# A graph-attention step whose gathers are released from ten places of VectorE's program instead of six places of two engines

## The chip, the cores and the metric

One core of one Trainium2 chip runs the whole kernel. The metric is device time in microseconds, from launch to the last output row, and the time before is the median of three runs: 2590.57 us (2587.11 to 2598.71). The core has five engines with programs of their own: TensorE (matmuls; PE in the profile, PEld for its weight loads), VectorE (DVE), ScalarE (ACT), GpSimd (POOL) and SyncE (SP, which only issues DMAs here). Each works through its program in order; they meet at semaphores.

## The reference

There are 6250 nodes with 64 values each, and 206250 edges sorted by destination (`dst`), each with 64 attributes.

```python
Qh = (x @ Wq.T + bq).reshape(n, H, D)          # H = 4 heads of D = 16
Kh = (x @ Wk.T + bk).reshape(n, H, D)
Vh = (x @ Wv.T + bv).reshape(n, H, D)
Ee = (edge_attr @ We.T + be).reshape(-1, H, D)
score = (Kh[src] * Qh[dst] * (1.0 / np.sqrt(D)) * Ee).sum(-1)
score = jnp.exp(jnp.clip(score, -5.0, 5.0))
msg = Vh[src] * score[..., None]
wV = jax.ops.segment_sum(msg, dst, num_segments=n)
x = _layernorm(x + wV)
```

So for every edge a row of keys and values is picked by `src` (an irregular index), a row of queries by `dst` (a slowly growing one), and the messages are added up by `dst`.

## The kernel before

*Setup.* TensorE makes a table `kv_tab` in HBM with 128 floats (key and value) for each node, and a query table. The edges are cut into 1612 tiles of 128, the tiles into groups of 8 (`G`), the groups into 105 steps (`STEPS`): 97 steps of two groups, 16 tiles, and eight of one group at the end.

*Gathers.* For a tile of 128 edges `gather_kv` (L450) issues one indirect DMA from GpSimd (L452): it reads 128 indices, one in each partition, and brings 128 rows of `kv_tab` into the tile's column of one of five buffers `kvs` (`KVB`). Step s issues the gathers of step s + 4, whose buffer step s - 1 has just given up. Not all of a step's 16 tiles are gathered: the last two or three of the second group are "picked" (below), and in each sixth step one tile comes row by row through SyncE (`fetch_rows`, L617). That leaves 14, 13 or 12.

*Release.* The gathers' indices lie in `src_i` from the start. So that a gather is not issued at once, an engine copies the columns that are due from `src_i` to `due_i` (L593 on VectorE, L595 on ScalarE), and the gathers read `due_i`: the place of this copy in its engine's program decides when they may start. `PARTS` cuts a step's 16 tiles in six parts; parts 0 to 2 are copied by VectorE, parts 3 to 5 by ScalarE. GpSimd itself does nothing else in the loop.

*A step on the engines.* The order of each engine's program is written out by hand in the loop over s (L793 to L874); an engine does what concerns it in that order.

- VectorE: the two products of the scores (`products`, L680 and L681, in place over keys, queries and edge values), the sum over the picked rows (`picked`, L553; in each fifth step also L546), the sum over the heads and the clip (`scores`, L687 and L689), two additions into the destinations' ring (`add`, L730), the message (L697), then one-hot matrices: two `hot` (L525), the destinations' one-hot (L663), two more `hot` (another two in each fifth step); then now and then the closing of a block of output.
- ScalarE: the squares (L650) and the rest (L655) that make the queries' one-hot `to` out of `pb`, the exponential (L690), the bias of the edge values (L642), the split of the message in three bf16 parts (L700, then L710 twice, with a matmul L708 ahead of each), a copy of the turned picked rows (L563), the picked rows' keys and values (L580).
- TensorE: the previous step's sums over destinations (L716), small transposes (L515), the spread of the destinations over partitions (`spread`, L628, into `pb`), the picks (below), the edge values (`edges`, L441, 16 matmuls), L708, the picked rows through the weights (L573, L575), the queries (`queries`, L673, 16 matmuls).
- Picks: two tiles of a step (three in each fifth) are not gathered but made by TensorE: the `hot` matrices select rows of x in 2 x 25 matmuls for each tile (`picks`, L539), in 100 matmuls a step (150 in each fifth).

L680 of the next step needs L673's queries and L580's rows; L553 needs the last picks; L650 needs L628; L710 needs L708; the last `hot` of a step needs a buffer that 25 picks have read.

Of the kernel before, what the change touches and what calls it, by code (L numbers as in the profile page):

```python
# [21 lines left out]
G = 8  # L22
# [16 lines left out]
KVB = 5  # L39
# [14 lines left out]
def tiles_in(s):  # L54
    return sum(tiles_of(g) for g in groups_of(s))
# [8 lines left out]
LAST = NS - 8 - 1  # L64
PARTS = 0, 2, 4, 7, 9, 11, 16

# [48 lines left out]
def tile_gnn(ctx: ExitStack, tc: tile.TileContext, x, xT, wT, bias, beT, weT, eT, src, dst, dst_rows,  # L115
             src_rows, out):
    nc = tc.nc
# [345 lines left out]
    with tc.If(rv == 0) as branch:  # L463

        with tc.tile_pool(name="work", bufs=2) as work, \
# [115 lines left out]

            def gather(s, part):

                if s >= NS:
                    return
                t0, n = STEPS[s][0] * G, tiles_in(s)
                lo, hi = PARTS[part] * n // 16, PARTS[part + 1] * n // 16
                todo = [t for t in range(t0 + lo, t0 + hi) if not is_picked(t // G, t % G)
                        and not (is_rowed(s) and t - t0 == COLUMN)]
                if todo:  # L590
                    due = slice(todo[0], todo[-1] + 1)
                    if part < 3:
                        nc.vector.tensor_copy(due_i[:, due], src_i[:, due])  # L593
                    else:
                        nc.scalar.activation(due_i[:, due], src_i[:, due], AF.Copy)  # L595
                for t in todo:
                    gather_kv(t // G, t % G, due_i)
# [79 lines left out]
            def products(s):  # L677
                n = tiles_in(s)
                prod = work.tile([P, 2 * G, C], F32, name="prod", bufs=1)
                nc.vector.tensor_mul(prod[:, :n, :], kvs[s % KVB][:, :n, :C], PQ[s][:, :n, :])  # L680
                nc.vector.tensor_mul(prod[:, :n, :], prod[:, :n, :], PE[s][:, :n, :])  # L681
                return prod

            def scores(s, prod):
# [3 lines left out]
                                        axis=AX.X, op=OP.add)  # L688
                nc.vector.tensor_scalar(score, score, -5.0, 5.0, op0=OP.max, op1=OP.min)  # L689
                nc.scalar.activation(score, score, AF.Exp)  # L690
                return score
# [101 lines left out]
            for s in range(NS):  # L793
# [14 lines left out]
                prod = products(s)  # L808
                gather(s + KVB - 1, 0)
                picked(s - 1)  # L810
# [4 lines left out]
                score = scores(s, prod)  # L815
                gather(s + KVB - 1, 1)
                if more:
                    biases(s + 1)
                    onehot_rows_rest(nexts[0])
                if s:  # L820
                    add(s - 1)
                msg = message(s, score)
                gather(s + KVB - 1, 2)
                if nexts[1:]:
# [3 lines left out]
                minus(s, msg, 0)  # L828
                gather(s + KVB - 1, 3)
                if nexts[1:]:  # L830
                    onehot_rows_rest(nexts[1])
                hots(s, 1, 0)
                picks(s, 0, 1)
                picked_turned(s - 1)
                minus(s, msg, 1)
                gather(s + KVB - 1, 4)
                if not more:

                    close(B - 2)
                    spreads(B - 2)  # L840
                hots(s, 1, 1)
                picks(s, 1, 0)
                picked_kv(s - 1)
                gather(s + KVB - 1, 5)
                sources(s + 1, 1)
                sources(s + 2, 0)
                sources(s + 1, 2)
                if more:
                    rows_fetched(s + 1)
                    if nexts[0] * G % KEYS == 0:  # L850
                        keys(nexts[0] * G)
                    onehot_edges(s + 1)
                    queries(s + 1)
                picks(s, 1, 1)
                for h in range(2):
                    hots(s, 2, h)
                for h in range(2):
                    picks(s, 2, h)
                hots(s + 1, 0, 0)
                hots(s + 1, 0, 1)  # L860
                if more:

# [188 lines left out]
```

## Time and profile before

| | |
|---|---|
| median of 3 runs | 2590.57 us (2587.11 to 2598.71) |
| the profiled execution | 2600.91 us |
| its span, first to last instruction | 2598.9 us |
| mean granted TensorE clock | 0.877 |
| first start of L680 / last | 144.6 us / 2586.1 us |
| busy: TensorE, VectorE, GpSimd, ScalarE | 1975.9, 1633.1, 1308.6, 1037.3 us |

The profile shows one execution. A row such as `L452 POOL DMA_INDIRECT kv<-kv_tab,due_i x1325 | 1250.9, 944 | 1212.2 <-...` names line, engine, operation, what is written and read, how often; then busy time, mean ns of one, idle time of the engine just ahead of it, and what ended most of that. A row of the timeline has the start and the length in us, engine, line, operation, what it writes and reads, how many were merged, and in brackets the engine's idle time ahead of it with its releaser. "issue" is a wait that nothing in the profile explains; "remote" and "another core or an unknown queue" mean that a semaphore came, but not just after any instruction that sets it. GpSimd's row for a gather covers the making of its transfer, not the transfer.

### The profile page before, as it was taken

To read this page: it belongs to the slowest core of one execution; us is meant where nothing else is said; L and a number is where in the kernel's file an instruction comes from. 1 tells how busy PE (TensorE), PEld (TensorE's weight loads), DVE (VectorE), ACT (ScalarE), POOL (GpSimd) and SP (SyncE) were. 2 spreads that over 40 slices of the span, in tenths; PEclk is the share of its full clock that TensorE was granted. 3 is DMA by queue.
4 is the path that set the end of the run, shared out by engine and by line. 5 is a ranking of instruction groups with operands and counts; after the bars stand their busy time and mean duration, and the time that the engine had idled before them with its cause. 6 is when DMAs were issued, how large, how long until landed. Compare 5 with 4: busy or idle time off the path is not lost.

```text
span 2598.9 us, 48744 instructions
## 1 busy us (share of the span) xinstructions
PE 1975.9 (76%) x17255; PEld 1622.2 (62%) x17255; DVE 1633.1 (63%) x2106; ACT 1037.3 (40%) x1793; POOL 1308.6 (50%) x1396
## 2 busy tenths in 40 slices
PE   4587887777877877777777777877777877877884
PEld 4466666666766666666666666666666666656663
DVE  3366666566665766766656656566666665756774
ACT  1344333344343434433434334343444443433454
POOL 4335554545554545545554545555545554555442
PEclk9979888888988989888988888888988988889995
DMA  4312221212222222222222222222222222222221
GB/s 125 115 35 65 59 64 54 64 53 68 64 64 54 67 54 67 60 63 65 55 64 62 58 63 54 64 64 55 72 57 64 67 58 62 58 62 65 60 57 37
DMA packets 108379, 163.46 MB, mean 63 GB/s; under 512 B 68825, under 2 KB 71084, under 8 KB 108012
## 3 DMA queue, kind: packets, MB, share of 16 engines
q0 software_dynamic: 44288, 89.74, 13.1%
q1 hardware_dynamic: 63452, 69.51, 9.5%
q8 instruction: 137, 2.24, 0.4%
q10 hardware_dynamic: 384, 1.00, 0.2%
q14 instruction: 118, 0.97, 0.1%
HBM read 152.80 MB, written 7.33 MB: 62 GB/s over the span
## 4 chain that ended last, share of the span: by engine, by line
PE 50%; issue 15%; another core or an unknown queue 12%; ACT 10%; DVE 8%; POOL 5%; DMA 1%; DVEq 0%; SPq 0%; ACTq 0%; POOLq 0%
PE pick L539 22%; PE pe L441 7%; POOL kv L452 5%; PE pb L539 4%; PE pq L708 4%; PE small L716 3%; ACT msg L710 2%; PE pb L575 2%; DVE small L687 2%; ACT pe L642 2%; DVE prod L680 2%; PE pq L673 2%; PE pb L628 2%; DVE prod L681 2%
## 5 line engine op out<-in xcount | busy, mean ns | idle before, releaser
L452 POOL DMA_INDIRECT kv<-kv_tab,due_i x1325 | 1250.9, 944 | 1212.2 <-DVE due_i L593 427.2
L539 PEld LDWEIGHTS <-hot 128*128 128x128 bf16 x10650 | 980.9, 105 | 470.8 <-issue 404.3
L539 PE MATMUL pick<-parts,hot 128*128 128x192 bf16 x9700 | 1008.0, 261 | 240.9 <-issue 168.2
L525 DVE TENSOR_TENSOR hot<-small,block 128x3200 bf16<-128x3200 bf16 x426 | 755.9, 1814 | 40.4 <-PE pick L539 15.0
L650 ACT ACTIVATE to<-pb,minus_row 126x1024 bf16<-126x1024 f32 x202 | 224.3, 1111 | 912.4 <-PE pb L628 441.6
L680 DVE TENSOR_TENSOR prod<-kv,pq 128x1024 f32<-128x1024 f32 (+2 forms) x105 | 123.6, 1177 | 419.4 <-ACT kv L580 94.4
L441 PE MATMUL pe<-we_sb,et 128*128 128x128 f32 x1612 | 261.8, 319 | 79.1 <-ACT pe L642 43.3
L441 PEld LDWEIGHTS pe<-we_sb,et 128*128 128x128 f32 x1612 | 236.3, 226 | 130.7 <-ACT pe L642 75.2
L710 ACT ACTIVATE msg<-pq 128x1024 bf16<-128x1024 f32 (+2 forms) x210 | 207.3, 987 | 162.3 <-remote 46.4
L655 ACT ACTIVATE to<-to,one_p 126x1024 bf16<-126x1024 bf16 x202 | 230.0, 1138 | 0.1
L687 DVE TENSOR_REDUCE small<-prod 128x64 f32<-128x1024 f32 (+2 forms) x105 | 123.9, 1180 | 130.0 <-remote 78.5
L716 PE MATMUL small<-msg,of 128*128 128x192 bf16 x1612 | 173.5, 260 | 28.6 <-issue 28.0
L628 PE MATMUL pb<-key_rows,ident_b 112*128 112x512 bf16 x403 | 136.4, 419 | 71.9 <-ACT to L650 42.8
L708 PE MATMUL pq<-msg,minus_b 128*128 128x512 bf16 x404 | 143.7, 435 | 55.4 <-ACT msg L710 47.7
L716 PEld LDWEIGHTS <-of 128*128 128x128 bf16 x1612 | 145.8, 104 | 42.7 <-issue 40.6
L539 PE MATMUL pb<-parts,hot 128*128 128x192 bf16 x950 | 122.1, 288 | 52.7 <-issue 51.8
L553 DVE TENSOR_REDUCE xp<-pick 128x128 f32<-128x384 f32 x97 | 53.6, 553 | 161.6 <-remote 105.5
L580 ACT ACTIVATE kv<-pb 128x256 f32<-128x256 f32 (+1 forms) x97 | 39.3, 405 | 227.1 <-PE pq L673 81.0
L681 DVE TENSOR_TENSOR prod<-prod,pe 128x1024 f32<-128x1024 f32 (+2 forms) x105 | 123.6, 1177 | 4.0
L697 DVE TENSOR_TENSOR pq<-kv,small 128x1024 f32<-128x1024 f32 (+2 forms) x105 | 123.3, 1174 | 0.1
L663 DVE TENSOR_TENSOR of<-small,key 128x2048 bf16<-128x2048 bf16 (+2 forms) x105 | 122.9, 1170 | 0.6 <-DVE key L448 0.3
L700 ACT ACTIVATE msg<-pq 128x1024 bf16<-128x1024 f32 (+2 forms) x105 | 103.9, 989 | 1.4 <-DVE pq L697 1.4
(141 smaller groups left out, 1314.5 us busy)
## 6 DMA issues: line engine op xcount, KB each, us to landing
et<-in_eT SPq DMA_DIRECT2D x100, 512.0 KB
rk<-kv_tab SPq DMA_DIRECT2D x1920, 0.5 KB
kv<-kv_tab,due_i POOLq DMA_INDIRECT x1325
qw<-q_tab SPq DMA_DIRECT2D x202, 15.8 KB
kv_tab<-kv_sb SPq DMA_DIRECT2D x5, 640.0 KB
q_tab<-q SPq DMA_DIRECT2D x5, 480.0 KB
acc<-in_x SPq DMA_DIRECT2D x48, 32.0 KB
out<-y SPq DMA_DIRECT2D x48, 32.0 KB
```

The source lines that it names most:

```text
L441: nc.tensor.matmul(pe[:, 2 * u:2 * u + 2, :], et[:, u, :], we_sb, start=False, stop=u == n // 2 - 1, skip_group_check=True)
L452: nc.gpsimd.indirect_dma_start(out=kv_of(g)[:, j, :], out_offset=None, in_=kv_tab[:, :], in_offset=bass.IndirectOffsetOnAxis(ap=of[:, t:t ...
L525: nc.vector.tensor_tensor(HOT[s, i, h].rearrange("p b (a c) -> p b a c", c=2), pairs(from_b[i])[:, None].to_broadcast(shape), block2[:, bl ...
L539: nc.tensor.matmul(to, hot[:, k, :], parts[:, b], start=b == 0, stop=b == NB - 1)
L628: nc.tensor.matmul(pb[:, b:b + 4, :], ident_b[:NR2, g // 2:g // 2 + 1].to_broadcast([NR2, P]), key_rows[:, g % 2, b * P:(b + 4) * P], star ...
L650: nc.scalar.activation(TO[g][:, :n, :], pb[:3 * W, :n, :], AF.Square, bias=minus_row3[:3 * W])
L655: nc.scalar.activation(TO[g][:, :n, :], TO[g][:, :n, :], AF.Relu, bias=one_p[:3 * W], scale=-1.0)
L680: nc.vector.tensor_mul(prod[:, :n, :], kvs[s % KVB][:, :n, :C], PQ[s][:, :n, :])
L687: nc.vector.tensor_reduce(score, prod[:, :n, :].rearrange("p g (h d) -> p g h d", h=H), axis=AX.X, op=OP.add)
L708: nc.tensor.matmul(msg[:, lo:hi, :], minus_b, M3[s][:, lo:hi, i, :], start=False, stop=True, skip_group_check=True)
L710: nc.scalar.activation(M3[s][:, :n, i + 1, :], msg[:, :n, :], AF.Copy)
L716: nc.tensor.matmul(PA[s], OH[s][:, j, :], M3[s][:, j], start=j == 0, stop=j == n - 1)
```

## The change

The six parts become ten places, with shares in `PLACES`; all copies are VectorE's. The gathers that are left after the picked and the row-wise tiles are taken out are now what is divided, so that a step with 14 has 1, 2, 1, 1, 1, 2, 1, 1, 2, 2 of them at the ten places. Places 0 and 1 stand behind the two products, 2 behind the clip, 3 behind the additions, 4 behind the message, 5 and 6 behind the two `hot` of the middle, 7 behind the destinations' one-hot, 8 and 9 behind the last two `hot`. No other work is moved, and the gathers' order on GpSimd within a step, tile by tile, stays.

```diff
-PARTS = 0, 2, 4, 7, 9, 11, 16
+PLACES = 1, 2, 1, 1, 1, 2, 1, 1, 2, 2
...
-            def gather(s, part):
+            def gather(s, place):
                 if s >= NS:
                     return
-                t0, n = STEPS[s][0] * G, tiles_in(s)
-                lo, hi = PARTS[part] * n // 16, PARTS[part + 1] * n // 16
-                todo = [t for t in range(t0 + lo, t0 + hi) if not is_picked(t // G, t % G)
+                t0 = STEPS[s][0] * G
+                todo = [t for t in range(t0, t0 + tiles_in(s)) if not is_picked(t // G, t % G)
                         and not (is_rowed(s) and t - t0 == COLUMN)]
+                lo, hi = (sum(PLACES[:k]) * len(todo) // sum(PLACES) for k in (place, place + 1))
+                todo = todo[lo:hi]
                 if todo:
                     due = slice(todo[0], todo[-1] + 1)
-                    if part < 3:
-                        nc.vector.tensor_copy(due_i[:, due], src_i[:, due])
-                    else:
-                        nc.scalar.activation(due_i[:, due], src_i[:, due], AF.Copy)
+                    nc.vector.tensor_copy(due_i[:, due], src_i[:, due])
                 for t in todo:
                     gather_kv(t // G, t % G, due_i)
...
                 nc.vector.tensor_mul(prod[:, :n, :], kvs[s % KVB][:, :n, :C], PQ[s][:, :n, :])
+                gather(s + KVB - 1, 0)
                 nc.vector.tensor_mul(prod[:, :n, :], prod[:, :n, :], PE[s][:, :n, :])
+                gather(s + KVB - 1, 1)
...
                 nc.vector.tensor_scalar(score, score, -5.0, 5.0, op0=OP.max, op1=OP.min)
+                gather(s + KVB - 1, 2)
                 nc.scalar.activation(score, score, AF.Exp)
...
                 prod = products(s)
-                gather(s + KVB - 1, 0)
...
                 score = scores(s, prod)
-                gather(s + KVB - 1, 1)
...
                     add(s - 1)
+                gather(s + KVB - 1, 3)
                 msg = message(s, score)
-                gather(s + KVB - 1, 2)
+                gather(s + KVB - 1, 4)
...
                 minus(s, msg, 0)
-                gather(s + KVB - 1, 3)
...
                 hots(s, 1, 0)
+                gather(s + KVB - 1, 5)
                 picks(s, 0, 1)
                 picked_turned(s - 1)
                 minus(s, msg, 1)
-                gather(s + KVB - 1, 4)
...
                 hots(s, 1, 1)
+                gather(s + KVB - 1, 6)
                 picks(s, 1, 0)
                 picked_kv(s - 1)
-                gather(s + KVB - 1, 5)
...
                     onehot_edges(s + 1)
+                    gather(s + KVB - 1, 7)
                     queries(s + 1)
...
                 hots(s + 1, 0, 0)
+                gather(s + KVB - 1, 8)
                 hots(s + 1, 0, 1)
+                gather(s + KVB - 1, 9)
```

## The prediction

> **What bounds the kernel now.** I read the page first: busy shares, then the chain of waits.
>
> ```profile
> PE 1975.9 (76%) x17255; PEld 1622.2 (62%) x17255; DVE 1633.1 (63%) x2106; ACT 1037.3 (40%) x1793; POOL 1308.6 (50%) x1396
> PE 50%; issue 15%; another core or an unknown queue 12%; ACT 10%; DVE 8%; POOL 5%; DMA 1%; DVEq 0%; SPq 0%; ACTq 0%; POOLq 0%
> L452 POOL DMA_INDIRECT kv<-kv_tab,due_i x1325 | 1250.9, 944 | 1212.2 <-DVE due_i L593 427.2 <-ACT due_i L595 412.9 <-issue 332.8
> ```
>
> No engine is full. TensorE work is half of the chain, and 27% of it is "issue" and "unknown queue": some 700 us in which engines waited for something that the page can't name. There is only one core, so the second name is a label. The timeline shows what these waits go with. First the stretch from 1300 us:
>
> ```profile
> 1302.98 0.94 POOL L452 DMA_INDIRECT kv<-kv_tab,due_i  x1 [3.44 <-ACT due_i L595]
> ...
> 1310.14 0.60 PE L628 MATMUL pb<-key_rows,ident_b 112*128 112x512 bf16 x2
> ...
> 1310.81 0.95 POOL L452 DMA_INDIRECT kv<-kv_tab,due_i  x1 [0.30 <-issue]
> 1313.11 0.56 DVE L553 TENSOR_REDUCE xp<-pick 128x128 f32<-128x384 f32 x1 [4.58 <-remote]
> 1313.33 1.11 ACT L650 ACTIVATE to<-pb,minus_row 126x1024 bf16<-126x1024 f32 x1 [7.21 <-remote]
> ...
> 1315.41 0.94 POOL L452 DMA_INDIRECT kv<-kv_tab,due_i  x1 [3.65 <-DVE due_i L593]
> ```
>
> Seven gathers run back to back from 1302.98 to 1311.76. ScalarE's L650 needs the matmul L628, over at 1310.74; VectorE's L553 needs picks over at 1308.9. Both start only at 1313.1 to 1313.3, some 1.4 us after the last gather of the run. TensorE's signals are held while gathers follow each other closely, and come out when the run ends. Then a longer run, ten gathers from 1432.49 on:
>
> ```profile
> 1437.80 1.38 PE L441 MATMUL pe<-we_sb,et 128*128 128x128 f32 x10
> 1439.66 0.27 PE L441 MATMUL pe<-we_sb,et 128*128 128x128 f32 x1 [0.48 <-issue]
> ...
> 1441.10 0.36 PE L441 MATMUL pe<-we_sb,et 128*128 128x128 f32 x1 [0.46 <-issue]
> ...
> 1442.50 0.27 PE L441 MATMUL pe<-we_sb,et 128*128 128x128 f32 x1 [1.04 <-issue]
> ...
> 1443.73 0.95 POOL L452 DMA_INDIRECT kv<-kv_tab,due_i  x1 [0.30 <-issue]
> 1445.37 0.37 PE L441 MATMUL pe<-we_sb,et 128*128 128x128 f32 x1 [1.77 <-issue]
> 1446.92 1.82 DVE L525 TENSOR_TENSOR hot<-small,block 128x3200 bf16<-128x3200 bf16 x1 [1.81 <-PE pe L441]
> 1446.97 1.11 ACT L650 ACTIVATE to<-pb,minus_row 126x1024 bf16<-126x1024 f32 x1 [7.19 <-PE pe L441]
> ...
> 1449.36 0.95 POOL L452 DMA_INDIRECT kv<-kv_tab,due_i  x1 [4.69 <-ACT due_i L595]
> ```
>
> TensorE does ten L441 matmuls in 1.38 us and then crawls, one in 0.5 to 1.8 us, until the run is over at 1444.68; L650 and the last `hot` wait 2.3 us beyond it. I counted both effects over the whole timeline. Idle time ("issue") ahead of an L539 matmul per gather, by the gather's place in its run: 0.00 us (first), 0.04, 0.02, 0.13, 0.26, 0.49 and 1.18 (seventh). A held signal never outlasted a pause on POOL of 1.8 us or more between two gathers (end to start) and was let out in only 3 of 18 pauses of 0.5 to 0.9 us. So what costs is a long unbroken run; one or two gathers cost little. After 200 us, with pauses under 0.7 us joined, there are 63 runs of seven, 71 of five, 53 of four, 45 of two, and only seven of eight or more.
>
> **The change, part by part.** A step's 14 gathers (13 or 12 in some) were released at three places on VectorE (2, 2, 3) and three on ScalarE (2, 2, 3). Now all are released by VectorE, 1, 2, 1, 1, 1, 2, 1, 1, 2, 2.
>
> (a) *Index copies.* VectorE has 951 instead of 301: 650 x 0.168 us (L593: 50.5 us for 301) = 109 us. VectorE is idle 37% of the time, mostly ahead of L680 (419 us of idle), which hides it; without that cover it is the 109 us. ScalarE loses L595, 60.5 us; it is 40% busy, so I take 0, at best 60.5 us.
>
> (b) *Who gates a gather.* ScalarE's places stand behind L710 and L580, which wait for TensorE's signals. While a run holds these, ScalarE can't release the next gathers: the runs end themselves, and the second fence ends with such a pause (4.69 us). VectorE's stretch from `scores` to the last `hot` waits on TensorE only once (the last `hot`, L525). That brake goes. A copy queues nothing new behind it; POOL's order stays step by step, and its waits on the landings of earlier gathers and SP's queue are as before.
>
> (c) *How long the runs get.* A gather occupies POOL 0.944 + 0.30 = 1.25 us, and starts some 0.34 us after its copy does (1314.98 to 1315.41, 1336.68 to 1337.11: 0.43 at most). VectorE's rows: product 1.23, L681 1.22, L553 0.55, L687 1.22, L689 0.23, two L730 about 0.8, L697 1.22, `hot` 1.81, L663 1.22, a copy 0.17. From the start of L680, no signal late, the gathers begin at 1.6 (place 0), 2.8 and 4.1 (1), 5.3 (2), 6.6 (3), 7.8 (4), 9.1 and 10.3 (5), 11.6 (6), 12.9 (7), 14.4 and 15.7 (8). From place 5 to 9 VectorE has four `hot`, one L663 and copies, about 9 us, for eight gathers, 10 us of POOL: POOL can't catch up. The only pause over 0.3 us is 0.6 ahead of place 8, too short. That is a run of twelve (ten or eleven if L553 waits and breaks it once), where before had seven and five.
>
> (d) *What a run of twelve does.* By the counts above TensorE crawls from its fifth gather (6.6 us) to its end at 16.6 plus about 1 us. L441 begins at about 6.5 and so ends near 18, and L708 follows; L650, L710 and the last `hot` get their signals at 16.6 + 2.3 = 18.9. From there, by rows of full-speed stretches: L650 1.1, L710 1.0, L708 0.6, 25 picks 2.2, the picked rows' matmuls 0.9, L673 0.65; with the 0.2 to 0.3 that lies between two, the next L680 is at 25.7. If the last `hot`'s signal is out in time, the last two gathers join the run (fourteen, to 19.1), all waits move 2.3 us, and the next L680 is at 28.0. Each fifth step has 50 picks more (4.4 us), 0.9 a step: 26.6 to 28.9 against 24.6 (mean between starts of L680 over the 92 steps from the fourth on): +2.0 to +4.3.
>
> The trace's own long runs bound it from below: the four steps that open with a run of nine or ten (its start at 489, 1432, 1708 and 1982 us) took 23.5, 25.4, 25.6 and 26.4 us, where steps of their place in the cycle of five average 22.8, 24.2, 23.9 and 22.8: +0.7 to +3.6, mean +1.8. So +0.7 and +4.3 are the ends, and I take +2.0, the hand-worked lower end, since it lies next to the measured mean.
>
> *Sum.* 93 steps release a two-group step's gathers: 93 x 2.0 = +186 us; (a) hidden. The profiled execution's own time is 2600.9 (span 2598.9 and 2.0 around it), 10 above the median 2590.6. 2601 + 186 = 2787, on the median's scale 2777: I say **2775**. The ends: 93 x 0.7 gives 2656, 93 x 4.3 gives 2990.
>
> One rule weighed here. The Trainium skill, "SBUF — State Buffer", section "SBUF: two separate sides", says engine ports and DMA ports are disjoint, so neither's work slows the other. By that rule a gather in flight could not disturb a matmul, where it is released would not matter, and the sum would be that of (a) alone. The L441 rows above, 0.14 us apart and then 0.5 to 1.8, do not agree.
>
> **The rivals.**
>
> *Short runs (faster).* If the spaced releases do leave pauses that let signals out, at 1 us or so, most steps become like the best of before, which begin at 1334.3, 1355.8 and 1483.3 and take 21.5, 20.6 and 20.8. For it: signals in the first two gathers of a run are mostly prompt, and a lone gather held one signal in 25. Against: VectorE's distances, 1.2 to 2.0 us per one or two gathers, are hardly above POOL's 1.25. It decides if the pace from place 2 on falls to one gather in 2.7 us (0.94 + a pause of 1.8). All steps at 21 + 0.9 would be -2.7 x 93 = -250 (2340); half of them, 2465. I price it at 2465.
>
> *Gathers are harmless, only copies count.* Then the signals' delay is something that merely coincides with runs, and the time is 2591 with the copies hidden to 2700 with all 109 us exposed; near 2600.
>
> *The change does not space anything* because POOL's backlog carries over each step: runs over fourteen, TensorE crawls all the time. POOL needs 17.5 us of 24.6, so a carried backlog would drain at the wait ahead of L680; if not, the step is the 28.9 or more, 2990.
>
> **Chances.** Longer runs 0.66 (2656 to 2900), the carried backlog 0.06, harmless gathers 0.06 (same 0.04, slower 0.02), short runs 0.22. Measured runs spread from 2587 to 2599, so 0.5% is about what can be told from no change. Faster 0.22, same 0.04, slower 0.74. The likeliest case's own range is 2656 to 2900. For 8 in 10 I leave out the faster half of the short runs and the far end of the backlog: 2450 to 2960.
>
> **What would show it.** Right, if L593 stands at 951 and L595 is gone; POOL's idle time ahead of L452 is put down to L593, with unbroken runs of ten or more in most steps; PE's "issue" ahead of L441 and L539 grows from its 624 us (L539), and L650's 912 us of idle too; L680 to L680 is 26 to 28 us. Wrong, if the runs stay at five or fewer: then "unknown queue" falls below 12% of the chain and steps shorten. If runs are long and the time is not, the crawl falls where TensorE waits for ScalarE anyway, which would sink step (d).

## The result, and the profile after

The changed kernel takes 2842.8 us (median of four, 2839.2 to 2859.0) where the kernel before takes 2589.4 (median of four executions, the three named above and one more): a ratio of 1.098, 95% interval 1.093 to 1.103, or +253 us. The profiled execution took 2843.4 us (span 2841.6) at a mean granted TensorE clock of 0.824, where it was 0.877 before. The direction was forecast, and the time is inside the range, but 68 us above the 2775 that was named.

The page of the changed kernel: the busy times, the chain of waits, and the groups that the prediction spoke of (busy time and mean ns, then idle time ahead of them and what ended most of it). After the change, L648, L678 and L711 are the lines that were L650, L680 and L710.

```profile
PE 2035.5 (72%) x17255; PEld 1640.8 (58%) x17255; DVE 1674.7 (59%) x2756; ACT 1015.2 (36%) x1491; POOL 1311.1 (46%) x1396
...
PE 58%; issue 20%; another core or an unknown queue 8%; ACT 8%; DVE 5%; POOL 1%; DMA 0%; POOLq 0%; DVEq 0%; SPq 0%; ACTq 0%
...
L452 POOL DMA_INDIRECT kv<-kv_tab,due_i x1325 | 1253.5, 946 | 1449.4 <-DVE due_i L593 1103.2
...
L539 PE MATMUL pick<-parts,hot 128*128 128x192 bf16 x9700 | 1101.8, 269 | 408.0 <-issue 398.2
...
L648 ACT ACTIVATE to<-pb,minus_row 126x1024 bf16<-126x1024 f32 x202 | 224.2, 1110 | 880.0 <-PE pb L626 477.2
L678 DVE TENSOR_TENSOR prod<-kv,pq 128x1024 f32<-128x1024 f32 (+2 forms) x105 | 123.6, 1177 | 606.9 <-ACT far L509 213.0
...
L563 ACT ACTIVATE xe<-pb 128x128 f32<-128x128 f32 x97 | 26.9, 277 | 445.1 <-remote 428.6
...
L593 DVE COPY due_i<-src_i 128x1 int32<-128x1 int32 (+2 forms) x951 | 154.0, 163 | 0.0
```

And of the kernel before:

```profile
L539 PE MATMUL pick<-parts,hot 128*128 128x192 bf16 x9700 | 1008.0, 261 | 240.9 <-issue 168.2
...
L650 ACT ACTIVATE to<-pb,minus_row 126x1024 bf16<-126x1024 f32 x202 | 224.3, 1111 | 912.4 <-PE pb L628 441.6
L680 DVE TENSOR_TENSOR prod<-kv,pq 128x1024 f32<-128x1024 f32 (+2 forms) x105 | 123.6, 1177 | 419.4 <-ACT kv L580 94.4
...
L563 ACT ACTIVATE xe<-pb 128x128 f32<-128x128 f32 x97 | 26.5, 273 | 111.5 <-remote 79.0 <-PE pick L539 20.9 <-PE pb L560 8.9
```

The reader is to see three things. The same instructions run: L452 has 1325 gathers of 946 ns, where they took 944. TensorE has 60 us more "busy" time at a lower clock, and it sits idle 408 us ahead of the picks of L539, nearly all of it "issue", where it was 241. And ScalarE sits idle 445 us ahead of L563, which waits for TensorE's transpose L560 (each fifth step also L562), where it was 112. The loss lies in the loop: from the start of one L678 to the next, a step takes 27.30 us on average where it took 24.63, and 2.67 x 95 steps is 253 us.

The lower clock is a small part of this. A pick starts 0.08 us behind the one before it at full pace (granted clock 1.00) and 0.16 us behind it at half pace (0.50). The trace after the change has 1561 starts of the second kind and the one before 1114, and 447 x 0.08 us is 36 us. L441 has fewer starts at half pace than before (168 against 356, some 0.1 us each, 19 us). These two are estimates from the starts in the two traces.

Where a step loses its time is seen in the timeline (start, duration, engine, instruction, and in brackets the idle time before it with what ended it):

```profile
1401.83 0.94 POOL L452 DMA_INDIRECT kv<-kv_tab,due_i  x1 [9.93 <-DVE due_i L593]
...
1405.25 2.23 PE L539 MATMUL pick<-parts,hot 128*128 128x192 bf16 x25
...
1407.42 0.27 PE L562 MATMUL pb<-ident,xp 128*64 128x128 f32 x1
...
1407.96 1.43 PE L539 MATMUL pick<-parts,hot 128*128 128x192 bf16 x15
...
1414.06 0.32 PE L539 MATMUL pick<-parts,hot 128*128 128x192 bf16 x1 [1.63 <-issue]
1414.60 0.94 POOL L452 DMA_INDIRECT kv<-kv_tab,due_i  x1 [0.30 <-issue]
...
1416.23 0.32 PE L539 MATMUL pick<-parts,hot 128*128 128x192 bf16 x1 [1.85 <-issue]
...
1417.72 0.28 ACT L563 ACTIVATE xe<-pb 128x128 f32<-128x128 f32 x1 [9.99 <-remote]
```

POOL issues eleven gathers from 1401.83 to 1415.55. The first 25 picks take 2.23 us. The next 25 begin at 1407.96, go at full speed for 15, and need until 1417.98 for the last ten, one to three at a time. The transposes of L560 and L562 are over at 1407.69, but ScalarE's L563, which waits for them alone, starts at 1417.72: ten us later, and 2.2 us after the run's end. That is the crawl and the held signal that the prediction described, in a longer run. Counted over the timeline after 200 us, idle time ("issue", over 0.2 us each) ahead of the matmuls of L539 and L441 was 248 us before and is 477 us after. This sum is called the crawl below. Put down to the last gather issued before the matmul, 271 us of the 477 lie at the eighth gather of a run or later, where it was 19.

### The profile page after: what moved, and what is told of

The parts are those of the page before. It is cut to its first block, busy times and chain, and to the rows that moved or that the text cites. A ratio compares the mean times of both kernels' runs of the same rounds, so it can differ in the third digit from the quotient of the medians.

```text
span 2841.6 us, 49443 instructions
## 1 busy us (share of the span) xinstructions
PE 2035.5 (72%) x17255; PEld 1640.8 (58%) x17255; DVE 1674.7 (59%) x2756; ACT 1015.2 (36%) x1491; POOL 1311.1 (46%) x1396
## 4 chain that ended last, share of the span: by engine, by line
PE 58%; issue 20%; another core or an unknown queue 8%; ACT 8%; DVE 5%; POOL 1%; DMA 0%; POOLq 0%; DVEq 0%; SPq 0%; ACTq 0%
PE pick L539 28%; PE pe L441 5%; PE small L717 5%; PE pq L709 4%; PE pb L539 4%; PE pb L575 3%; PE pb L626 3%; PE pq L671 2%; DVE small L687 2%; ACT pe L640 2%; ACT msg L711 1%; ACT to L653 1%; ACT to L648 1%; ACT msg L701 1%
## 5 line engine op out<-in xcount | busy, mean ns | idle before, releaser
L452 POOL DMA_INDIRECT kv<-kv_tab,due_i x1325 | 1253.5, 946 | 1449.4 <-DVE due_i L593 1103.2
L539 PEld LDWEIGHTS <-hot 128*128 128x128 bf16 x10650 | 1014.6, 107 | 673.3 <-issue 596.4
L539 PE MATMUL pick<-parts,hot 128*128 128x192 bf16 x9700 | 1101.8, 269 | 408.0 <-issue 398.2
L525 DVE TENSOR_TENSOR hot<-small,block 128x3200 bf16<-128x3200 bf16 x426 | 769.5, 1817 | 109.7 <-remote 87.5
L648 ACT ACTIVATE to<-pb,minus_row 126x1024 bf16<-126x1024 f32 x202 | 224.2, 1110 | 880.0 <-PE pb L626 477.2
L678 DVE TENSOR_TENSOR prod<-kv,pq 128x1024 f32<-128x1024 f32 (+2 forms) x105 | 123.6, 1177 | 606.9 <-ACT far L509 213.0
L441 PE MATMUL pe<-we_sb,et 128*128 128x128 f32 x1612 | 226.2, 292 | 87.7 <-ACT pe L640 50.5
L441 PEld LDWEIGHTS pe<-we_sb,et 128*128 128x128 f32 x1612 | 201.7, 200 | 134.2 <-ACT pe L640 85.5
L711 ACT ACTIVATE msg<-pq 128x1024 bf16<-128x1024 f32 (+2 forms) x210 | 207.2, 987 | 161.7 <-remote 65.2
L687 DVE TENSOR_REDUCE small<-prod 128x64 f32<-128x1024 f32 (+2 forms) x105 | 124.3, 1184 | 152.4 <-PE pick L539 54.6
L563 ACT ACTIVATE xe<-pb 128x128 f32<-128x128 f32 x97 | 26.9, 277 | 445.1 <-remote 428.6
L593 DVE COPY due_i<-src_i 128x1 int32<-128x1 int32 (+2 forms) x951 | 154.0, 163 | 0.0
L539 PE MATMUL pb<-parts,hot 128*128 128x192 bf16 x950 | 113.9, 278 | 52.6 <-issue 52.4
L626 PE MATMUL pb<-key_rows,ident_b 112*128 112x512 bf16 x403 | 125.3, 392 | 29.9 <-ACT to L648 27.9
L680 DVE TENSOR_TENSOR prod<-prod,pe 128x1024 f32<-128x1024 f32 (+2 forms) x105 | 123.6, 1177 | 1.8
L698 DVE TENSOR_TENSOR pq<-kv,small 128x1024 f32<-128x1024 f32 (+2 forms) x105 | 123.4, 1176 | 0.2 <-issue 0.2
L671 PEld LDWEIGHTS <-to 126*128 126x128 bf16 x1612 | 81.9, 116 | 57.4 <-issue 47.5
```

The costliest lines, as they stand in the source:

```text
L441: nc.tensor.matmul(pe[:, 2 * u:2 * u + 2, :], et[:, u, :], we_sb, start=False, stop=u == n // 2 - 1, skip_group_check=True)
L452: nc.gpsimd.indirect_dma_start(out=kv_of(g)[:, j, :], out_offset=None, in_=kv_tab[:, :], in_offset=bass.IndirectOffsetOnAxis(ap=of[:, t:t ...
L525: nc.vector.tensor_tensor(HOT[s, i, h].rearrange("p b (a c) -> p b a c", c=2), pairs(from_b[i])[:, None].to_broadcast(shape), block2[:, bl ...
L539: nc.tensor.matmul(to, hot[:, k, :], parts[:, b], start=b == 0, stop=b == NB - 1)
L626: nc.tensor.matmul(pb[:, b:b + 4, :], ident_b[:NR2, g // 2:g // 2 + 1].to_broadcast([NR2, P]), key_rows[:, g % 2, b * P:(b + 4) * P], star ...
L648: nc.scalar.activation(TO[g][:, :n, :], pb[:3 * W, :n, :], AF.Square, bias=minus_row3[:3 * W])
```

## The experiments

The rival explanations were: (A) long unbroken runs of gathers on POOL make TensorE crawl and hold its signals back, so what counts is how the gathers are strung; (B) the 650 extra VectorE copies; (C) the gathers cost what they cost, however strung.

One thing has to be known to read them. The chips on which they ran fall into two kinds. On chips 9 and 11 the kernel before takes 1768 to 1769 us; on chips 1, 5 and 7 it takes 2557 to 2592, like the executions that the prediction was made from. Each result below is a ratio to the kernel before on its own chip, and the expectations name the case that they were written for.

**Chips 9 and 11.** Four kernels ran on chip 9. Seven idle copies a step added to the kernel before, the release places left alone:

```diff
+            def idle(s, place):
+                if s < NS:
+                    t0, n = STEPS[s][0] * G, min(PLACES[place], tiles_in(s))
+                    nc.vector.tensor_copy(idle_i[:, :n], src_i[:, t0:t0 + n])
...
+                idle(s + KVB - 1, 3)
                 msg = message(s, score)
```

> The kernel before with its six release places, plus seven idle index copies on VectorE in each step (one or two columns each, into a tile that nobody reads), at the places where the changed kernel has copies and the old one has none. So VectorE has the changed kernel's number of copies and the gathers are released as before. Theory of the runs: the copies hide in VectorE's idle time, 2580 to 2620 us, and runs of gathers stay at seven and five. Rival (the extra copies on VectorE are what costs): some 650 x 0.165 us = 107 us on the path, 2660 to 2700, or all of the loss, 2840.

The changed kernel with the copies of places 5 to 9 on ScalarE:

```diff
-                    nc.vector.tensor_copy(due_i[:, due], src_i[:, due])
+                    if place < 5:
+                        nc.vector.tensor_copy(due_i[:, due], src_i[:, due])
+                    else:
+                        nc.scalar.activation(due_i[:, due], src_i[:, due], AF.Copy)
```

> The changed kernel with the same ten places in the text, but the copies of places 5 to 9 (eight of 14 gathers) by ScalarE, where they stand behind instructions that wait for TensorE (L711, L563, L580). Theory of the runs: the brake is back, runs of eleven go, and the time returns to 2560 to 2680 us. Rival (the finer spread as such, one or two gathers at a time, is what costs): still 2800 or more. Rival (VectorE's copies): 475 copies fewer of 0.163 us, 2765 us.

The changed kernel with a pause on POOL after every fourth gather:

```diff
                     gather_kv(t // G, t % G, due_i)
+                    issued[0] += 1
+                    if issued[0] % 4 == 0:
+                        for _ in range(4):
+                            nc.gpsimd.iota(pause_i, pattern=[[1, 224]], base=0, channel_multiplier=0)
```

> The changed kernel with a pause on GpSimd after every fourth gather of the loop: four iotas of 128x224 (0.32 us of work each, so some 1.5 to 2.5 us). All release places, copies and gathers stay; GpSimd has more to do, 3.5 pauses a step, in all about 24 us a step. Theory of the runs: an unbroken run can't be longer than four, TensorE's signals come out in each pause, and the time falls to 2600 to 2700 us though GpSimd works more; idle time of 'issue' ahead of L539 on TensorE falls below half of 398 us. Rival (GpSimd's sheer activity, or a port that it shares with VectorE, is what costs): 2840 or slower.

And the changed kernel without the loop's gathers:

```diff
-                for t in todo:
-                    gather_kv(t // G, t % G, due_i)
```

> The changed kernel without the gathers of the loop: the copies stay at their ten places, the rows of keys and values stay those of the first steps, so the output lacks the right keys and values. Theory of the runs: TensorE's signals come out at once and it never crawls; the page's unknown queue falls below 3% of the chain, a step takes what TensorE and its partners need, 19.5 to 21.5 us, 2200 to 2400 us in all. Rival (gathers in flight don't disturb the engines, as a rule has it that ports of engines and DMAs are apart): 2800 to 2850 us.

Measured, beside a kernel before of 1768.1 us: idle copies 1782.8 (1.010, 1.007 to 1.013), half on ScalarE 1769.0 (1.000, 0.998 to 1.003), pause 2280.4 (1.292, 1.289 to 1.296), no gathers 1766.3 (0.998, 0.996 to 1.000). On this chip (A) fails: taking every gather away gained nothing, and pausing cost 512 us. The expectations in microseconds missed, since they were written for a kernel before of 2590. The kernel with half of the copies on ScalarE, which was to test whether waits on ScalarE brake the gathers, ran on this chip alone, where there is nothing to brake. The next two kernels then ran on chip 11: the changed kernel unaltered, and seven places of two gathers, each behind an instruction that waits for TensorE.

> The changed kernel unaltered, on the chip that the experiments get. The first experiments ran on a chip on which the kernel before takes 1768 us, and its profile there shows no held signals at all. Theory of the runs, as it now stands (the cost of a long run is that TensorE's signals are held, which only happens where the traces show it): on a chip without holds the change costs its index copies only, VectorE being 94% busy there, 1.00 to 1.02 times the kernel before; on a chip with holds (kernel before near 2590) it is 1.08 to 1.12 times. Rival (long runs cost the same everywhere, through GpSimd or through VectorE's order): 1.08 or more on either chip, 1910 or more where before takes 1768.

```diff
-PLACES = 1, 2, 1, 1, 1, 2, 1, 1, 2, 2
+PLACES = 2, 2, 2, 2, 2, 2, 2
...
+                    if place == 0:
+                        nc.vector.tensor_copy(due_i[:, due], src_i[:, due])
+                    else:
+                        nc.scalar.activation(due_i[:, due], src_i[:, due], AF.Copy)
...
                 minus(s, msg, 0)
+                gather(s + KVB - 1, 3)
```

> A step's gathers two at a time from seven places, each behind an instruction that waits for a signal of TensorE: one on VectorE (behind L553), six on ScalarE (behind both L648, both L711, L563 and L580 of the changed kernel's numbering). Theory of the runs: where signals are held, a run ends after two to four gathers because the next release needs a signal, and the time is below before's, 2350 to 2550 against 2590; where they are not held, 0.99 to 1.01 times before. Rival (the harm lies in how finely the gathers are spread): as slow as the changed kernel, 1.08 or more.

Measured, beside 1769.1 us: the changed kernel 1779.5 (1.006, 1.004 to 1.008), gated pairs 1769.7 (1.000, 0.998 to 1.002). So on this kind of chip the same change costs 10 us, not 253. The page of the changed kernel on chip 11, and then its timeline:

```profile
PE 1662.0 (94%) x17255; PEld 1460.9 (82%) x17255; DVE 1656.1 (93%) x2756; ACT 1009.2 (57%) x1491; POOL 1308.5 (74%) x1396
```

```profile
1006.20 0.95 POOL L452 DMA_INDIRECT kv<-kv_tab,due_i  x1 [0.30 <-DMA kv<-kv_tab,due_i]
...
1006.58 2.05 PE L441 MATMUL pe<-we_sb,et 128*128 128x128 f32 x16
1007.45 0.95 POOL L452 DMA_INDIRECT kv<-kv_tab,due_i  x1 [0.30 <-DMA kv<-kv_tab,due_i]
1008.51 1.11 ACT L648 ACTIVATE to<-pb,minus_row 126x1024 bf16<-126x1024 f32 x1
```

POOL strings its gathers together without a break over whole steps here, longer runs than anywhere else, and yet L441's sixteen matmuls take 2.05 us and L648 starts without an idle time worth a bracket. TensorE and VectorE are both busy 93 to 94% of the span, so the extra copies have little idle time to lie in: 10 us in the changed kernel, 15 us when added idly, none that can be measured when half of them move to ScalarE. That fits (B), and nothing else of the change shows on these chips.

**No gathers, and one release, on chip 5.** The kernel without gathers again, beside the changed kernel with its ten places made one:

```diff
-PLACES = 1, 2, 1, 1, 1, 2, 1, 1, 2, 2
+PLACES = 14,
...
-                gather(s + KVB - 1, 1)
```

> The changed kernel with one release place instead of ten: a single VectorE copy per step, behind the first of the three thirds of the products, releases all gathers of a step at once (95 copies at L593 instead of 951, and no ScalarE copies). The two theories part here. (A) The number of copies on VectorE is all that the change costs where no signals are held: the 856 copies of about 0.16 us that go take back the 10 us by which the changed kernel stood above the kernel before in the run with its ten places unaltered (1779.5 against 1769.1), so this one ends at 1760 to 1770 beside a kernel before of 1769, although its gathers now stand in one run of up to fourteen. (B) The length of the runs costs by itself, on every execution: then this kernel, whose runs are the longest of all, is slower than the changed kernel, at 1800 or more beside 1769. On an execution that holds TensorE's signals (a kernel before of about 2590), the prediction's mechanism says the longest runs cost most: step of 29 us or more and 2900 to 3050; copies alone would give 2590 there.

> The kernel without the loop's gathers once more (this part of the computation is left out: the products read what lies in the buffers), beside a kernel before on whatever execution this is. If the kernel before takes 1769 here, gathers cost nothing and it ends within 0.5% of 1766, as before. If the kernel before takes about 2590 here, the two theories part: if back-to-back gathers hold TensorE's signals and are the cause of those executions' length, the kernel without them falls by hundreds of microseconds, to 1800 to 2200; if something else of the chip or of the recording slows everything, it stays at 2500 or more.

Measured, beside 2557.1 us: without gathers 1823.0 (0.713, 0.709 to 0.717); one release 3208.6 (1.254, 1.249 to 1.260). Without gathers, by the page:

```profile
PE 1669.7 (92%) x17255; PEld 1464.1 (80%) x17255; DVE 1652.3 (91%) x2757; ACT 1009.2 (55%) x1491; POOL 57.5 (3%) x71
...
L541 PE MATMUL pick<-parts,hot 128*128 128x192 bf16 x9700 | 867.0, 246 | 35.7 <-DVE xp L555 35.4
```

The step is 16.55 us on chip 5 and 16.54 on chip 9: with the gathers gone, the two kinds of chip are the same in the loop. The 57 us that are left, 1823 against 1766, lie ahead of the loop: the first products begin at 143.6 us, where the kernels on chips 9 and 11 begin them between 79 and 89 us. That goes with gathers too. The setup keeps 59 of its own, in two unbroken runs of 32 and 27, and in the first run (2.83 to 42.67 us) ScalarE's copies L342 of TensorE's products wait like this:

```profile
19.20 0.38 ACT L342 ACTIVATE kv_sb<-ps 128x256 f32<-128x256 f32 x1 [6.67 <-remote]
28.30 0.38 ACT L342 ACTIVATE kv_sb<-ps 128x256 f32<-128x256 f32 x1 [8.72 <-remote]
38.81 0.38 ACT L342 ACTIVATE kv_sb<-ps 128x256 f32<-128x256 f32 x1 [10.12 <-remote]
```

On chip 9 the same copies of the same kernel wait 0.47 us each at first. So in a run this long signals come out within the run as well, one in some 10 us. On chip 5, then, some 734 us of the kernel before are the gathers' doing, though POOL has 1251 us of them in either case. And that the gathers' stringing decides is seen in the one release, which has 101 copies at L593 instead of 951 and the longest runs of this chip. Its page and a stretch of its timeline:

```profile
PE 2103.1 (66%) x17255; PEld 1720.7 (54%) x17255; DVE 1619.1 (51%) x1906; ACT 1022.2 (32%) x1491; POOL 1307.5 (41%) x1396
...
PE 55%; issue 21%; another core or an unknown queue 15%; ACT 5%; DVE 4%; DMA 0%; SPq 0%; DVEq 0%; ACTq 0%
...
L648 ACT ACTIVATE to<-pb,minus_row 126x1024 bf16<-126x1024 f32 x202 | 224.3, 1111 | 1653.1 <-remote 1075.5
L441 PE MATMUL pe<-we_sb,et 128*128 128x128 f32 x1612 | 385.3, 366 | 452.2 <-issue 411.4
```

```profile
2605.78 0.95 POOL L452 DMA_INDIRECT kv<-kv_tab,due_i  x1 [12.95 <-DVE due_i L593]
...
2615.12 1.86 PE L441 MATMUL pe<-we_sb,et 128*128 128x128 f32 x7 [0.44 <-ACT pe L640]
...
2618.57 0.37 PE L441 MATMUL pe<-we_sb,et 128*128 128x128 f32 x1 [1.05 <-issue]
...
2622.01 0.94 POOL L452 DMA_INDIRECT kv<-kv_tab,due_i  x1 [0.30 <-issue]
...
2624.15 0.37 PE L441 MATMUL pe<-we_sb,et 128*128 128x128 f32 x1 [1.73 <-issue]
...
2625.83 1.11 ACT L648 ACTIVATE to<-pb,minus_row 126x1024 bf16<-126x1024 f32 x1 [8.71 <-PE pe L441]
```

Fourteen gathers run from 2605.78 to 2622.95. Seven matmuls of L441 take 1.86 us (0.21 us from one to the next, where it was 0.11 on chip 11: the granted clock is 0.50 in this stretch), and then one comes every 1.4 to 2.1 us until 2.6 us after the run's end, when the last four come together. L648's idle time is 1653 us where the kernel before has 912. The expectation for a chip of this kind (2900 to 3050, steps of 29 us or more) was too low: 3209 and 30.94 us.

**Releases behind TensorE's signals, on chip 1.** The kernel of the gated pairs again.

> Seven places of two gathers once more, each behind an instruction that waits for TensorE's signal (six of the seven copies on ScalarE), on whatever execution this is. Where the kernel before takes 1769, it stays at 1765 to 1775 as it did. Where the kernel before takes about 2560 to 2590, the theories part. (A) What costs is how many gathers follow one another before POOL pauses, and a release that waits for TensorE keeps that number small, since a held signal holds the next release too: runs of two to five, steps of 20 to 23.5 us, and 2150 to 2500, below the kernel before. (B) It is the number of gathers in a step, or their bytes, however they are strung: 2560 to 2600, the kernel before's own time. (C) Any release that is spread further than the kernel before's five or six batches lengthens the runs: 2750 to 2900, like the ten places.

Measured: 2548.0 beside 2592.4 (0.985, 0.979 to 0.990). It is a little faster, by less than 2%, and none of the three expectations held. Its (A), below the kernel before, is 48 us away, and its (B), the kernel before's own time, 12 us, so this kernel doesn't part the two. The timeline says why:

```profile
1409.02 0.19 ACT L596 ACTIVATE due_i<-src_i 128x2 int32<-128x2 int32 x1
1409.47 0.94 POOL L452 DMA_INDIRECT kv<-kv_tab,due_i  x1 [2.48 <-ACT due_i L596]
1410.01 0.20 ACT L596 ACTIVATE due_i<-src_i 128x2 int32<-128x2 int32 x1
...
1411.30 0.21 ACT L596 ACTIVATE due_i<-src_i 128x2 int32<-128x2 int32 x1
...
1412.46 0.20 ACT L596 ACTIVATE due_i<-src_i 128x2 int32<-128x2 int32 x1
...
1420.94 0.38 ACT L580 ACTIVATE kv<-pb 128x256 f32<-128x256 f32 x1 [8.28 <-remote]
```

When TensorE's signals come out, several come within a few microseconds, four gates open within 3.6 us, and eight gathers follow one another from 1409.47 to 1419.17; the next signal is held again. 79 of this kernel's runs are of eight. So gates that wait for TensorE didn't keep the runs short here.

**Pauses on POOL, on chip 5.** The kernel that added four iotas (1.48 us) after every fourth gather again, and then with two (0.72 us):

> The changed kernel with four short iotas on POOL (about 1.5 us busy) after every fourth gather, once more: some 5 us of work a step are added to the engine that issues the gathers, and nothing is taken away. Where the kernel before takes 1769 it gave 2280, since POOL then needs about 24 us a step and bounds the kernel. Where the kernel before takes 2540 to 2600 the theories part. (A) The cost sits in the gathers behind the fourth of a run, and a pause lets TensorE's signals out: runs of four, the crawl ahead of the pick's matmuls falls from 477 us (changed kernel) to below 150, and POOL's own 24 us a step are all that is left: 2300 to 2450, below both kernels although work was added. (B) The pauses are too short to let anything out, or the number of gathers and not their stringing counts: 2800 to 3100, the changed kernel's time plus part of the added 500 us of POOL work.

> The changed kernel with two iotas after every fourth gather instead of four, so a pause of about 0.75 us where it was 1.5 us; POOL then needs about 20 us a step. On an execution whose kernel before takes 2540 to 2600: (A) if what frees TensorE's signals is any pause between groups of four, the step falls to POOL's 20 us or so and the kernel to 2130 to 2250, below the 2336 of the pause of 1.5 us. (B) The prediction joined gathers less than 0.7 us apart into one run and saw signals come 1 to 2.3 us after a run's end; if a pause must last that long to let them out, the runs join, the crawl ahead of the pick's matmuls comes back (250 us or more) and the kernel takes 2500 to 2900. Where the kernel before takes 1769: POOL-bound, 1900 to 2050.

Measured: with 1.48 us, 2336.3 beside 2563.0 (0.912, 0.907 to 0.917); with 0.72 us, 2567.9 beside 2564.7 (1.001, 0.998 to 1.004). The page of the longer pause:

```profile
PE 1804.8 (77%) x17255; PEld 1557.9 (67%) x17255; DVE 1663.2 (71%) x2756; ACT 1017.5 (44%) x1491; POOL 1729.8 (74%) x2720
...
L452 POOL DMA_INDIRECT kv<-kv_tab,due_i x1325 | 1250.1, 943 | 474.9 <-issue 351.2
L539 PE MATMUL pick<-parts,hot 128*128 128x192 bf16 x9700 | 972.0, 261 | 295.3 <-DVE xp L553 235.6
...
L602 POOL IOTA pause_i<- 128x224 int32 x1324 | 422.1, 319 | 70.8
```

422 us of work were added to the engine that issues the gathers, and the kernel became faster than the kernel before by 227 us. The crawl counted as above is 67 us, against 477 in the changed kernel. L452 no longer waits for a release (474.9 us of idle, mostly "issue", where the changed kernel has 1449.4 on the copies): POOL is seldom out of work, and its own 21.9 us a step are the bound (21.95 on chip 9). That is also why the same kernel is 29% slower on chip 9, where there is nothing to gain. The shorter pause, in its timeline:

```profile
1414.22 0.95 POOL L452 DMA_INDIRECT kv<-kv_tab,due_i  x1 [0.30 <-issue]
...
1415.18 0.71 POOL L602 IOTA pause_i<- 128x224 int32 x2
1416.29 0.95 POOL L452 DMA_INDIRECT kv<-kv_tab,due_i  x1 [0.40 <-DVE due_i L596]
...
1419.85 0.19 PE L678 MATMUL pq<-qw,to 126*128 126x64 bf16 x1 [0.43 <-issue]
...
1421.98 0.21 PE L678 MATMUL pq<-qw,to 126*128 126x64 bf16 x1 [1.07 <-issue]
...
1422.14 0.38 ACT L580 ACTIVATE kv<-pb 128x256 f32<-128x256 f32 x1 [3.47 <-remote]
```

(This profiled execution took 2542.6 us, 25 less than the kernel's median.) A group of four ends at 1415.16, the next runs from 1416.29 to 1420.99, and TensorE crawls through it and through the pause behind it; ScalarE's L580 has waited 3.47 us when it starts 1.1 us after the group. The crawl adds up to 176 us, less than the 250 that the expectation named. With its pause a group takes 5.8 us and POOL could do a step in about 20, but the step is 24.2. From one gather's end to the next one's start the long pause is mostly 1.9 or 1.65 us and the short one 0.9 or 1.1. Somewhere between them lies what lets TensorE's signals out on this chip; the prediction's count in the trace of before (no held signal outlasted a pause of 1.8 us) agrees.

**The copies, on chip 7.** The kernel before with the idle copies again.

> The kernel before with seven idle VectorE copies a step added (650 copies of about 0.16 us, 105 us of VectorE's time, no release moved), once more. Where the kernel before takes 1769 it cost 1.0%. Where the kernel before takes 2540 to 2600, VectorE is busy 63% of the time and waits for TensorE's signals anyway: (A) the prediction took the copies as hidden there, so ratio 0.995 to 1.01, at most 25 us, and nearly all of the changed kernel's 253 us is the gathers' stringing. (B) A third or more of the copies lies on the path that sets the end, because VectorE's work starts only when a late signal comes and everything behind it shifts: ratio 1.015 to 1.045, 40 to 110 us, and the stringing is charged with so much less.

Measured: 2588.4 beside 2589.2 (0.999, 0.996 to 1.002).

```profile
PE 1964.1 (76%) x17255; PEld 1618.8 (63%) x17255; DVE 1676.3 (65%) x2813; ACT 1041.8 (40%) x1793; POOL 1311.0 (51%) x1396
```

VectorE is busy 65% here where it was 94% on chip 9, and the 707 added instructions cost nothing. So the copies have no part in the 253 us that this could see: the interval of the ratio is 11 us less to 5 us more. That rules (B) out on this chip.

The executions side by side, for the chips of the slower kind. Gathers less than 0.7 us apart count as one run. The steps of the kernel before and the changed one are those of the first executions; the ratio is to the kernel before on the same chip.

| kernel | gathers behind the fourth of their run | crawl, us | step, us | ratio to before |
|---|---|---|---|---|
| without gathers | 0 | 0 | 16.55 | 0.713 |
| pause 1.48 us | 0 | 67 | 21.92 (POOL's own) | 0.912 |
| gated pairs | 380 | 254 | 23.97 | 0.985 |
| pause 0.72 us | 0 (751 if joined under 1.2 us) | 176 | 24.22 | 1.001 |
| before, idle copies | 308 | 228 | 24.39 | 0.999 |
| before | 320 | 248 | 24.63 | 1 |
| changed | 534 | 477 | 27.30 | 1.098 |
| one release | 905 | 610 | 30.94 | 1.254 |

From before to changed, 214 more gathers stand behind a fourth, 2.3 a step, and the step is 2.67 us longer; from before to one release it is 585, 6.3 a step, and 6.31 us. That is 1.0 to 1.2 us for each gather that is strung on behind the fourth. It is a line through these two differences and not a rule. The gated pairs lie off it by about 1.3 us a step. The pause of 0.72 us doesn't lie on it however its runs are counted. And from no gathers to the kernel before the step grows by 8.1 us, with 3.4 gathers a step behind a fourth: at 1.0 to 1.2 us each, this count explains about half of what gathers cost the kernel before.

## Why the prediction was right, and where its sizes were off

*The mechanism.* Right on chips of the kind that the profile was taken on, and now shown from both ends: taking the gathers away takes 734 us away, breaking the runs makes the kernel faster although work is added, and one unbroken run a step costs 651 us with fewer copies. The rival that gathers are harmless and only copies count is out on chips 5 and 7, and is what chips 9 and 11 do. That gathers cost the same however strung, (C), is out on chip 5, where kernels with the same 1325 gathers take from 2336 to 3209 us. What in the chip holds the signals is not shown. The rule of the Trainium skill ("SBUF — State Buffer", section "SBUF: two separate sides"), that the engines' and the DMAs' ports don't get in each other's way, agrees with the trace of chip 11 (sixteen L441 in 2.05 us amid gathers). On chip 5 (one L441 in 1.4 to 2.1 us) TensorE does slow down while gathers are issued, and no run here tells whether that happens at these ports.

*Step (a), copies hidden.* Right: the idle copies gave 0.999. The condition named with it, "without that cover it is the 109 us", is met on chips 9 and 11, and there the price was 10 to 15 us, not 109. A copy's duration is not its price: the page has 103.5 us more of L593, but VectorE's busy time grew by 41.6 only (1633.1 to 1674.7), since the instruction behind a copy begins while the copy is still running (a copy of 0.14 us at 1402.44, the message L698 at 1402.50).

*Step (b), ScalarE's places as a brake.* Not borne out as it was reasoned. The gated pairs, with six of seven releases on ScalarE behind waits for TensorE, make runs of eight: there a gate that waits delays the start of a run and then lets everything through. That the runs of before stay at seven may then only be because ScalarE's three places, like VectorE's, hold seven gathers together; that was not tested.

*Step (c), the length of the runs.* The main line said twelve, the parenthesis "ten or eleven if L553 waits and breaks it once". The parenthesis happened: places 0 and 1 make a run of three, the third's reduction and L687 wait, and places 2 to 9 make a run of exactly eleven in 45 of 86 steps counted.

*Step (d), what it costs.* This is the term of the sum that was mis-sized: +2.0 us a step was taken and +2.67 was measured, between its ends of +0.7 and +4.3. The lower end of the working by hand was chosen because the trace's own four long runs averaged +1.8. Those were runs of nine and ten; a fifth, ten gathers from 590.4 us, begins 0.5 us ahead of its step and isn't among the four, and that step took 23.7 us where its place averages 23.9. The working by hand is also summed too low: its rows, 1.1 to 0.65, add up to 6.45 us, which with 18.9 is 25.35, so that 25.7 has room for one or two gaps of 0.2 to 0.3 us and not for the five between six rows. With five it is 26.35 to 26.85, and +2.65 to +3.15 where +2.0 stands. That the measured +2.67 lies at the edge of this is in part luck: the 45 steps that open a run of eleven take 29.1 us, 0.2 beyond the hand-worked upper end of 28.9, and 40 others with a run of four to ten or of twelve average 25.8, so half of the steps pay 4.5 us and half pay 1.2 (the same against steps of their own place in the cycle of five). The mean over steps of two kinds came near a value that neither kind has. By the cycle of five steps, the place that was longest pays most (27.88 to 33.44 us), three pay 1.3 to 4.1, and one gains (24.49 to 23.49).

*What would show it.* L593 at 951, L595 gone, POOL's idle time put down to L593 (1103 of 1449 us), steps of 27.3: all as said. L539's "issue" idle time by its own view went from 624 to 1047 us. Two signs were wrong. L650 (now L648) did not wait longer: 880 us against 912; the waits grew at L563 and at L678 (419 to 607), because it is the picks that fall into the long run here, and L441 that falls into it in the one release, where L648 does wait 1653. And "unknown queue" was given as a share that falls when runs are short; it fell from 12% to 8% with longer ones, while "issue" rose from 15% to 20%. It would fall so if TensorE crawled until its own end, and no longer the signal behind it, was the wait; but with one release, the longest runs of all, the share is 15%. So it doesn't follow the length of the runs, and the reason stays open.

*What the prediction could not have.* All of its evidence came from one kind of execution. On the other kind the same diff is worth 0.6%, and nothing in a single profile says that there are two.

## What to carry to other kernels

Ahead of a change to when small gathers are issued, count the unbroken runs on the queue that issues them and look at what another engine does from the fifth on; a release that spreads gathers by hardly more than their own issue time (1.25 us here, releases 1.2 to 2.0 us apart) joined them into longer runs. Before a wait is explained by the kernel alone, run the kernel without the suspected work: one such run (1823 against 2557 us, and 1766 against 1768 on another chip) said more than all readings of the trace. And take a price from rows of the length that the change makes, not from the nearest shorter one, when the cost per item rises along the run.

## What the runs showed of the hardware

- The same kernel takes 1768 to 1769 us on two chips and 2557 to 2592 on three and in the first executions; on chip 5 it did so three times over. Without the loop's gathers the changed kernel takes 1766 us on one and 1823 on another, with the same step of 16.5 us, and the 57 us lie where the setup's own gathers run. So the difference is something that happens while gathers are under way. What sets the two kinds of chip apart was not found.
- A further difference of the two kinds stands in the traces' records of semaphore updates. On the eight semaphores of the gathers, the changed kernel's trace on chip 11 has 21,639 of them, 16 for each of 1352 gathers. The first executions have 6,610 (before) and 5,856 (changed), and the one release on chip 5 has 3,893. Whether the updates themselves are late or joined there, or only their records are lost, can't be read from a trace. Where records are missing, "issue" and "remote" can't be told from a wait whose update wasn't recorded; the idle time is there all the same. Every execution here lists its span and granted clock, so each was recorded, and what one without recording would do is not known: that the recording itself has a part in the crawl was not ruled out. That the path of semaphore updates is crowded would fit held signals, a TensorE that waits for nothing visible, and a cure by pauses; it is argued, not shown.
- On chip 5, pauses of 1.65 to 1.9 us between groups of four gathers free most of TensorE's crawl (67 us are left), and pauses of 0.9 to 1.1 us don't (176). Whether the bytes of a gather or its number of rows sets this was not tried.
